# Four edits in a fused four-layer convolution kernel: where a mean is taken off, a fused weighting and sum, the engine that writes zeroes, and the order of small matmuls

## The chip, the cores and the metric

The kernel runs on one core of a Trainium2 chip. The core has TensorE (PE in the profile; its weight loads are shown as PEld), VectorE (DVE), ScalarE (ACT), GpSimd (POOL) and SyncE (SP), which here only issues transfers. The metric is the device time of the whole kernel in microseconds (us), lower is better. The kernel before takes 7199.5 us, the median of 3 runs (7186.45 to 7207.52).

## The reference, cut to what matters

The input x has the shape (16, 32, 128, 128), fp32. Four layers follow, each `x = x + layer(groupnorm(x))`, where the group norm takes mean and variance over 2 channels and all of the image:

```python
x = x + _L0_conv_ref(_gn(x), ...)   # a row LSTM over the skewed image
x = x + _L1_conv_ref(_gn(x), ...)   # "adder" convolution: -sum |patch - w|
x = x + _L2_conv_ref(_gn(x), ...)   # Hartley transform, 32 x 32 modes mixed, back
x = x + _L3_conv_ref(_gn(x), ...)   # five edge filters, normed, then a small U-net
```

The change lies in layers 2 and 3. Layer 2 takes a two-dimensional Hartley transform of the normed image along both axes (a product with cos + sin), keeps the lowest 32 x 32 modes, adds a mirrored and signed copy, multiplies over the 32 input channels for each mode (the mixing), and transforms back:

```python
xm = dht2d(x)[:, :, :m1, :m2]
z = einsum('bixy,ioxy->boxy', xm, yeven) + einsum('bixy,ioxy->boxy', flip(xm), yodd)
out = dht2d(zero_padded(z)) / (h * w)
```

The constant mode of a transform is the plain sum; all its other modes do not see a constant that is added to the image.

Layer 3 starts with five edge filters, each normed by its own mean and standard deviation over the whole image (`b_k = (c_k - mean) / std`). The first convolution works on the five together. The kernel never forms the five filtered images: it takes products of the image's rows with its rows (a Gram matrix), and the variance of each filter is a weighted sum over that matrix. The normed filters are then folded into the weights of the first convolution.

## The kernel before, in words

**Stages.** `stage0` is the LSTM (to about 870 us). `Differences.run` is layer 1: for 16 images, two halves each, 72 differences of 128 x 8192 or 128 x 8320 fp16 elements per half are made, each by DVE (L708) or by ACT (L705), and summed by PE (L595). Layers 2 and 3 (`After`) run for four groups of four images each. The first three groups are woven into layer 1 as background work, the fourth (and what is left of the third) follows when layer 1 has ended, in `drain`. So there are a stage before, a combined stage and a tail.

**What sets the order.** In the combined stage a planner writes the order by hand. It keeps a model of the time of DVE, ACT and PE (`weave.dve`, `weave.act`, `weave.pe`). For each difference it estimates when DVE (2.36 us each) and ACT (7.15 us each) would be done and gives it to one of them. In between it advances `After.work`, a Python generator: what it yields is the time of a PE step (positive), a wait (negative) or a wait for sums, and its steps are emitted when the model says that PE has room. Every background operation adds its cost to the model by hand (`weave.dve += 2.2`). `keep_order` then fixes that order on each engine, so a changed cost moves later work. Where differences have no sum ready, `keep_busy` fills PE with products of zeroes (L625). In the tail `drain` runs the two generators (third and fourth group) side by side by the same model; each engine keeps its own order of instructions.

**Layer 2, `forward(g)`.** `xs` (128 x 4096 fp32) is the right side of the mixing: its two off-diagonal blocks must be zero, and POOL zeroes them (L988, L989). Eight tiles xh of 16 channels are loaded (L997). The group norm's statistics are computed on DVE and PE, spread to all partitions by a product (L1013) and copied to `mr` (L1015: mr[:, 0] the means, mr[:, 1] the inverse deviations). For each tile n: `centred` subtracts the mean from the 128 x 2048 tile in place on DVE (L1019); `first` transforms along the rows on PE (L1066), the result is copied to `ta` (L1070); `turned` transposes it on PE (L1081); `scaled` multiplies by the inverse deviation out of PSUM into t1, 16 channels by 32 modes (L1025); `second` transforms along the other axis (L1036). The modes are copied (L1040), stored to memory (L1046) and read back in another layout into xs and xw (L1119); an addition on DVE makes the mirrored part (L1126, L1133).

**Mixing.** For each of 32 ky, 16 products with 128 x 32 weights and 8 columns (L1154). The product k writes to the 32 partitions of column group j = k // 4 of the result, so four products in a row use the same column group of PE. Each fp32 product shows as two matmuls in the trace. The weights come in 8 tiles of four ky each (L1141). The result is copied (L1171) and stored (L1178).

**Layer 3, `statistics`.** Gram products on PE (L1354) into four PSUM banks, 420 columns each. For each of five filters and four banks the bank is multiplied by a table `gm` (L1414) and the product is summed over its columns (L1415) into `red`. Sums over partitions (L1424), mean, variance and inverse root follow on DVE; then `wf`, the folded weights (L1480, L1482), from tables v that POOL loads (L1467). `conv1` begins with L1627 and L1643, which need wf, and its main work is L1671. ACT normalises the frames that statistics and conv1 read (L1313 with copies at L1317 to L1320); small copies of their sides go to DVE (L1384).

## Time and profile before

The profiled execution has a span of 7206.6 us from its first to its last instruction; that is within the spread of the three runs and 7.1 us above their median.

| what | us |
|---|---|
| median of 3 runs | 7199.5 |
| lowest and highest run | 7186.45, 7207.52 |
| span of the profiled execution | 7206.6 |
| PE busy, in the whole span | 5631.0 |
| DVE busy | 5845.3 |
| ACT busy | 5498.0 |
| POOL busy | 111.8 |
| POOL's zeroing of xs (L988 and L989, eight operations) | 14.6 + 11.3 |

How to read it: busy time is a sum over the whole span and hides that the stages have different limits. In the stretch in which an engine is busy nearly all the time, work taken from it shortens the stretch; in a stretch in which it waits, it does not. So each part of the change has to be placed in its stretch first, and the waits there tell what it frees. The profile is one execution, so its durations are set against its own span.

### The profile page before, as it was taken

How to read it: one execution, taken by the hardware profiler on the slowest of the kernel's cores; microseconds unless marked ns; L12 is line 12 of the kernel's file. 1: busy time of each engine (PE TensorE's matmuls, PEld its weight loads, DVE VectorE, ACT ScalarE, POOL GpSimd, SP SyncE). 2: the span in 40 equal slices, each digit the busy share in tenths (PEclk: the TensorE clock that was granted, in tenths of full speed). 3: DMA queues.
4: the chain of work that ended last, by engine and by line, in shares of the span. 5: the costliest groups of instructions: out<-in, count | busy, mean ns of one | idle time of the engine just before them, and what ended most of it. 6: DMA issues, size and time to landing. Idle time of an engine off the chain costs nothing. (4 is left out here: it accounts for less than half of the span.)

```text
span 7206.6 us, 271424 instructions
## 1 busy us (share of the span) xinstructions
PE 5631.0 (78%) x127740; PEld 3001.3 (42%) x127740; DVE 5845.3 (81%) x7099; ACT 5498.0 (76%) x3100; POOL 111.8 (2%) x91
## 2 busy tenths in 40 slices
PE   4778567777877777998777787999776784797896
PEld 3665333333334343333334343333333443554564
DVE  7787689999998989999998999999998994134224
ACT  2555489999998989999999999999998991131222
POOL 0000000000000000000000001000000000000000
PEclk9899789999988898999888998999888986798997
DMA  8664211111133432221343343221252245252324
GB/s 310 230 205 144 83 63 57 55 58 47 47 101 93 141 98 81 63 69 47 78 126 98 115 118 104 65 65 46 57 134 92 64 136 150 89 170 74 86 51 98
DMA packets 372719, 722.57 MB, mean 100 GB/s; under 512 B 50896, under 2 KB 217296, under 8 KB 360720
## 3 DMA queue, kind: packets, MB, share of 16 engines
q1 hardware_dynamic: 364128, 670.79, 30.6%
q0 software_dynamic: 7040, 33.80, 1.4%
q8 instruction: 999, 16.37, 1.0%
q14 instruction: 120, 0.98, 0.0%
q10 hardware_dynamic: 432, 0.64, 0.0%
HBM read 507.28 MB, written 164.32 MB: 93 GB/s over the span
## 5 line engine op out<-in xcount | busy, mean ns | idle before, releaser
L705 ACT ACTIVATE d_act<-q,neg 128x8192 f16<-128x8192 f16 (+1 forms) x631 | 4462.6, 7143 | 184.4 <-PE acc L595 135.0
L708 DVE TENSOR_SCALAR d_dve<-q,qw 128x8192 f16<-128x8192 f16 (+1 forms) x1673 | 3859.4, 2362 | 200.8 <-PE acc L595 158.0
L595 PE MATMUL acc<-d_dve,sel 128*32 128x512 f16 x26768 | 1869.8, 402 | 504.0 <-DVE d_dve L708 454.0
L595 PEld LDWEIGHTS <-sel 128*32 128x32 f16 x36864 | 1026.9, 100 | 2164.4 <-issue 1507.8
L1671 PE MATMUL acc<-xp,wf 32*32 32x512 f32 x25600 | 1043.7, 618 | 37.6 <-issue 32.8
L595 PE MATMUL acc<-d_act,sel 128*32 128x512 f16 x10096 | 724.4, 408 | 356.2 <-ACT d_act L705 343.6
L1671 PEld LDWEIGHTS acc<-xp,wf 32*32 32x32 f32 x25600 | 431.9, 104 | 416.5 <-issue 329.6
L625 PE MATMUL acc<-q,zero 128*32 128x512 f16 x7248 | 522.9, 401 | 0.0
L1609 ACT ACTIVATE y<-pooled,b 32x128 f32<-32x128 f32 x488 | 195.0, 400 | 414.4 <-DVE pooled L1595 407.8
L207 PE MATMUL pg<-h,wb 64*64 64x20 f32 (+15 forms) x4096 | 395.7, 320 | 106.1 <-DVE h L256 64.8
L852 PE MATMUL acc<-y,u_conv 32*32 32x256 f32 (+1 forms) x9728 | 359.8, 459 | 76.0 <-issue 46.6
L244 ACT ACTIVATE gt<-pg,bias 128x20 f32<-128x20 f32 (+15 forms) x1024 | 315.8, 374 | 80.2 <-PE pg L207 73.1
L1313 ACT ACTIVATE xp<-xp,shift,stats 128x1280 f32<-128x1280 f32 (+1 forms) x128 | 182.6, 1434 | 240.5 <-DMA xp<-x_d 210.1
L207 PE MATMUL pg<-e,wb 64*64 64x20 f32 (+15 forms) x4096 | 353.1, 315 | 16.4 <-DVE e L260 5.4
L207 PEld LDWEIGHTS pg<-h,wb 64*64 64x64 f32 x4096 | 248.3, 154 | 140.7 <-DVE h L256 90.4
L625 PEld LDWEIGHTS <-zero 128*32 128x32 f16 x7248 | 218.6, 102 | 203.0 <-issue 46.1
L207 PE MATMUL pg<-xn,wb 64*64 64x28 f32 (+61 forms) x4096 | 284.5, 302 | 11.3 <-ACT gt L244 3.8
L207 PEld LDWEIGHTS pg<-e,wb 64*64 64x64 f32 x4096 | 251.5, 156 | 92.1 <-DVE e L260 62.9
L1354 PE MATMUL acc<-xp 32*64 32x204 f32 (+3 forms) x8576 | 238.5, 344 | 37.8 <-ACT xp L1319 28.8
L1800 DVE TENSOR_SCALAR s<-acc,l_ms,l_one 128x512 f32<-128x512 f32 x128 | 102.3, 824 | 199.0 <-PE acc L852 199.0
L255 ACT ACTIVATE th<-c 128x20 f32<-128x20 f32 (+15 forms) x256 | 81.3, 320 | 235.5 <-DVE c L253 234.1
L852 PEld LDWEIGHTS acc<-y,u_conv 32*32 32x32 f32 x9728 | 171.4, 110 | 196.6 <-issue 130.4
(215 smaller groups left out, 4303.1 us busy)
## 6 DMA issues: line engine op xcount, KB each, us to landing
xr<-x_d SPq DMA_DIRECT2D x192, 512.0 KB
xp<-x_d SPq DMA_DIRECT2D x112, 640.0 KB
q<-q_d SPq DMA_DIRECT2D x32, 2145.0 KB
x_d<-xr SPq DMA_DIRECT2D x128, 512.0 KB
x_in<-in_x_dram SPq DMA_DIRECT2D x16, 2048.0 KB
res<-in_x_dram SPq DMA_DIRECT2D x64, 512.0 KB
xn<-in_xs_dram SPq DMA_DIRECT2D x64, 512.0 KB
xn<-xn SPq DMA_DIRECT2D x128, 256.0 KB
```

Source lines behind the costliest of these rows:

```text
L207: nc.tensor.matmul(bank[c][q][64 * pair : 64 * pair + 64, :, :width], wb[half, 4 * kind + KIND[q]].rearrange("p b o -> p (b o)"), v[half], ...
L244: nc.scalar.activation(gt[:, q, :, :n], bank[c][q][:, :, :n], AF.Tanh if q == G else AF.Sigmoid, bias=bias[:, KIND[q] : KIND[q] + 1],)
L595: self.nc.tensor.matmul(acc[k][32 * j : 32 * j + 32, :], self.sel16[:, i // 9, :], d[:, row : row + 4, c : c + W], start=first, stop=last,)
L625: self.nc.tensor.matmul(acc[k][32 * j : 32 * j + 32, :], self.zero, q[:, :4, :W], start=False, stop=False)
L705: nc.scalar.activation(dst, src, AF.Relu, bias=self.neg[:, i : i + 1])
L708: nc.vector.tensor_scalar(dst, src, self.qw[:, i : i + 1], 0.0, ALU.subtract, ALU.max)
L852: nc.tensor.matmul(acc[blk][32 * j : 32 * j + 32, o : o + rows * n], t[part, 4 * par + tap, :], src[part, top : top + rows, left : left + ...
L1313: nc.scalar.activation(v, v, AF.Identity, bias=self.shift3, scale=self.stats3[:, 1])
L1354: nc.tensor.matmul(gram[blk][j : j + width, at : at + n], xp[part, l, 2 + j : 2 + j + width], xp[part, rows, j : j + width + 4], start=sta ...
L1609: nc.scalar.activation(d, s, AF.Identity, bias=bj)
L1671: nc.tensor.matmul(acc[blk][32 * j : 32 * j + 32, :], tap_of("all", tap)[rows], xp[rows, 4 * j + kh : 4 * j + kh + 4, kw : kw + W], start= ...
L1800: nc.vector.tensor_scalar(s.rearrange("p r w b -> p b r w"), acc[blk].rearrange("p (b r w) -> p b r w", b=2, w=64), istd[:, blk : blk + 1] ...
```

## The change

- `forward`, zeroes: two ACT activations per group replace the two POOL memsets; each reads one element of a constant over and over (step 0), multiplies it by 0.0 and writes 64 x 2048 elements. The model is charged 4.2 us on ACT.
- `forward`, mean: `centred` is gone. The first transform now sees the raw image. One operation makes mr[:, 0] = mean x 128 x inverse deviation, and after `scaled` a second small operation takes that off column 0 of each channel of t1, the constant mode of the first transform (16 elements on each partition).
- `statistics`: the multiplication and the reduction become one fused operation with an accumulator output; the compiled program has two instructions for it, the operation and a read of the accumulator. The model is charged 0.7 us instead of 1.2.
- `mixing`: the 16 products of one ky are issued in the order 0, 4, 8, 12, 1, 5, ..., so that the column group changes with each product.

```diff
@@ forward @@
-            nc.gpsimd.memset(xs[:64, 4:], 0.0)
-            nc.gpsimd.memset(xs[64:, :4], 0.0)
+            for part, off in ((slice(0, 64), xs[:64, 4:]), (slice(64, 128), xs[64:, :4])):
+                one = cst["ones"][part, 0:1]
+                flat = bass.AP(one.tensor, one.offset, [list(one.ap[0]), [0, 2048]])
+                nc.scalar.activation(off.rearrange("p b k y -> p (b k y)"), flat, AF.Identity, scale=0.0)
+            self.weave.act += 4.2
...
-                def centred(n):
-                    x, cs = xh[n], slice(16 * (n % 2), 16 * (n % 2) + 16)
-                    nc.vector.tensor_tensor(x, x, bcast(mr[:, 0, n // 2, cs], 2, W), ALU.subtract)
-                    weave.dve += 2.2
+
+                nc.vector.scalar_tensor_tensor(mr[:, 0], mr[:, 0], float(H), mr[:, 1], ALU.mult, ALU.mult)
 
                 def scaled(n, p):
                     cs = slice(16 * (n % 2), 16 * (n % 2) + 16)
@@ scaled @@
                         t1, p.rearrange("p (c k) -> p c k", k=M1), bcast(mr[:, 1, n // 2, cs], 2, M1), ALU.mult
                     )
-                    weave.dve += 0.7
+                    nc.vector.tensor_sub(t1[:, :, 0], t1[:, :, 0], mr[:, 0, n // 2, cs])
+                    weave.dve += 0.9
                     t1s[n] = t1
...
                 yield -4.0
-                centred(0)
-                yield -2.5
                 t1s, ta, ready = {}, {}, {}
...
                 for n in range(10):
-                    if n < 7:
-                        centred(n + 1)
                     if n < 8:
                         yield first(n)
@@ mixing @@
-            for k in range(16):
+            for k in [4 * j + i for i in range(4) for j in range(4)]:
                 j = k // 4
                 nc.tensor.matmul(
@@ statistics @@
                 w = pool.tile([128, GRAM], F32, name="es_w", bufs=1)
-                nc.vector.tensor_tensor(w, gram[blk][:, :GRAM], gm[k], ALU.mult)
-                nc.vector.tensor_reduce(red[:, blk, k : k + 1], w, AX.X, ALU.add)
-                weave.dve += 1.2
+                nc.vector.tensor_tensor_reduce(
+                    w, gram[blk][:, :GRAM], gm[k], 1.0, 0.0, ALU.mult, ALU.add, accum_out=red[:, blk, k : k + 1]
+                )
+                weave.dve += 0.7
                 if blk % 2:
                     yield -1.0
```

## The prediction

> **What bounds the kernel now.** I read the page first: its span, the busy shares and the 40 slices.

> ```profile
> span 7206.6 us, 271424 instructions
> ...
> PE 5631.0 (78%) x127740; PEld 3001.3 (42%) x127740; DVE 5845.3 (81%) x7099; ACT 5498.0 (76%) x3100; POOL 111.8 (2%) x91
> ...
> DVE  7787689999998989999998999999998994134224
> ACT  2555489999998989999999999999998991131222
> PEclk9899789999988898999888998999888986798997
> ```

> A slice is 180 us. DVE and ACT stand at 8 to 9 tenths from slice 5 to slice 33 and nearly empty afterwards: two stages with different limits. The start times of L708 and L207 give the borders (last LSTM product near 870 us, last difference near 5943), and the table of stretches gives their sums. Its columns are the stretch, its length, busy time and count of each engine, granted clock, DMA share, GB/s.

> ```profile
> 870.00:5943.40 5073.40, 4056.81 (x85506) 1904.30 (x85510) 4742.43 (x3860) 4801.01 (x1234) 91.48 (x51) 0.92 0.28 83
> 5943.40:7206.60 1263.20, 963.45 (x29938) 622.44 (x29930) 431.75 (x1033) 265.56 (x514) 17.85 (x33) 0.84 0.38 103
> ```

> In the combined stage (5073 us) DVE is busy 93.5% and ACT 94.6%: they share the same differences, so it ends when their joint work ends. In the tail (1263 us) PE works 963 us; it is limited by PE and, where PE is idle, by chains through DVE and DMA. The groups by shape give the prices (us busy, mean ns of one):

> ```profile
> L705 ACT ACTIVATE d_act<-q,neg 128x8192 f16<-128x8192 f16 x451 | 3186.8, 7112 | 155.0 <-PE acc L595 105.7 <-DMA q<-q_d 46.7 <-issue 1.8
> L708 DVE TENSOR_SCALAR d_dve<-q,qw 128x8192 f16<-128x8192 f16 x1085 | 2522.7, 2351 | 162.9 <-PE acc L595 120.9 <-DMA q<-q_d 40.1
> L1154 PE MATMUL acc<-xs,mix 128*32 128x8 f32 x4096 | 103.4, 186 | 46.3 <-DMA mix<-in_mix_dram 15.7 <-DMA q_d<-qt 13.4 <-DVE is_t L759 11.5
> L1019 DVE TENSOR_TENSOR xh<-xh,mr 128x2048 f32<-128x2048 f32 x32 | 72.5, 2285 | 4.2 <-DMA xh<-x_d 4.2
> L1414 DVE TENSOR_TENSOR es_w<-acc,gm 128x420 f32<-128x420 f32 x80 | 47.5, 594 | 12.5 <-PE acc L1354 9.4 <-DVE es_red L1415 0.5
> L1415 DVE TENSOR_REDUCE es_red<-es_w 128x1 f32<-128x420 f32 x80 | 47.2, 590 | 2.5
> ```

> Last the timeline of the tail, where the removed work meets PE's idle time (start, length, engine, instruction, in brackets idle before and what ended it):

> ```profile
> 6011.49 11.10 DVE L1019 TENSOR_TENSOR xh<-xh,mr 128x2048 f32<-128x2048 f32 x5
> 6022.66 6.69 DVE L1019 TENSOR_TENSOR xh<-xh,mr 128x2048 f32<-128x2048 f32 x3
> 6022.82 1.25 ACT L1313 ACTIVATE xp<-xp,shift,stats 128x1024 f32<-128x1024 f32 x1 [4.01 <-DVE sides L1384]
> 6029.42 1.28 DVE L1070 COPY ta<-acc 128x512 f32<-128x512 f32 x2
> 6030.16 1.12 PE L1081 MATMUL acc<-cw,ta 128*128 128x128 f32 x4 [11.76 <-DVE ta L1070]
> ...
> 6118.92 0.61 PE L1424 MATMUL acc<-es_red,cw 128*128 128x20 f32 x2 [26.85 <-DVE es_red L1415]
> 6131.47 11.85 PE L1154 MATMUL acc<-xs,mix 128*32 128x8 f32 x387 [11.53 <-DVE is_t L759]
> 6179.95 0.29 PE L1627 MATMUL acc<-cw,wf 128*32 128x4 f32 x8 [12.74 <-DVE wf L1482]
> 6204.80 10.76 PE L1671 MATMUL acc<-xp,wf 32*32 32x512 f32 x273
> ```

> PE stands behind the mean subtraction, then the Gram sums, then the mixing, then wf; only at 6204.8 does the long run of conv1 begin.

> [...] the trace's L1313 (1024: 1246 ns, 1280: 1461) [...] gives 2.1. [...] L1627 agrees: its eight, over four column groups, take 0.29 us in all.

> **The combined stage.** Counted in the built programs up to the last difference, three groups' transforms and two groups' Gram sums lie here.
> - DVE loses 24 subtractions x 2.285 = 54.8 us and 40 Gram pairs x (0.594 + 0.590) = 47.4, together 102.2.
> - DVE gains 40 fused operations. Nothing in the trace shows one. Lower bound 0.60 (the multiply alone, read hidden), upper 1.2 (half rate over its two streams, 0.594 + 0.44, plus a read of 0.17 like the smallest DVE operations, e.g. L739). I take 0.70, since it reads the same two streams as L1414: 28.0. Further 24 subtractions of 16 columns x 0.17 = 4.1, and three scalings of 128 columns x 0.28 (as L1040) = 0.8.
> - The planner hands 9 differences from ACT to DVE (L708 1682 for 1673, L705 622 for 631): +9 x 2.36 = 21.2 on DVE, -9 x 7.14 = -64.3 on ACT.
> - ACT gains six zeroings x 2.1 = 12.6 and one normalisation with its copies (1.9) that was in the tail.
> - Sum: DVE -102.2 + 54.1 = -48.1; ACT -64.3 + 14.5 = -49.8. Two engines that must end together agree. The fused operations now wait for one another on DVE, so I take **-46**. The idle rest (331 us of DVE) I leave unscaled: most waits are for sums at the borders of units. Bounds: -25 (fused at 1.2) to -58.

> Costed at nothing: the mixing here, because PE is not the limit (its 7248 filler products L625 become 7088); POOL's zeroing, 26 us busy on an idle engine. The zeroes on ACT have no wait of their own here; the differences queued behind them are delayed by what is already summed. If that cover fails (memory not free yet), ACT stalls with all differences behind it.

> **The tail**, by the changed kernel's order of instructions:
> 1. First transform. L1066 no longer needs the mean, and the ta copies come behind only the sides copies. The last of these needs L1313, which waited 4.01 us behind the subtractions; it could start at 6018.8 and be copied at 6021. So ta at about 6021 for 6029.4: **-8.5**. From there xm goes through SP to memory and returns as xs and xw; those DMA times stay, so mixing starts at 6123, not 6131.5.
> 2. Gram: 33 us (6085.3 to 6118.3) become 20 x 0.75 + 5 of other copies = 20, from 6077 to 6097. In the new order the last two mode additions follow the first pieces of wf, no longer inside the Gram block; wf is ready at about 6131.
> 3. Mixing: PE does 392 of 512 products before L1627, in 784 instructions. Before, 1024 took 35.5 us at half clock (30 ns each in the runs). L1627's eight start within 0.11 us, 14 ns each: 784 x 0.014 = 11 us. Bounds: 6 ns (the step between its neighbours) to 30. So L1627 at 6134 for 6180: **-46**. The mix weights of the last eight columns may hold it a little (before, the pair issued at 6135.66 filled the DMA until 6147).
> 4. The other 120 products come between conv1's (+3.5), and z then returns about 17 us after its copy, near 6202, when PE is there: +2.
> 5. Zeroes: ACT writes them near 5968, in a 25 us wait for a frame load; the loads into xs start near 6047. Nothing; with the cover gone, 4.2 us on the frames behind. POOL loses a wait of 61 us, but its next transfers (gm, v) wait for DVE anyway. SP keeps its order but for one frame load.
> 6. Last group's Gram (6579 to 6612) is 9 us shorter, and wf is waited for again (25.6 us in two times, 12.7 shown above); PE has conv2 beside it: -2.

> Sum -46 + 3.5 + 2 - 2, about **-42**. What is late next is PE itself: 201 of 210 us busy from 6240 to 6450. Bounds: -8.5 (only step 1) to -55.

> Together -88. The span, 7206.6, lies 7.1 above the median of the runs and inside their spread; I subtract from the median: 7199.5 - 88 = **7112**.

> **Rivals.**
> - Only the combined stage pays: the tail's DMA round trips decide, as the DVE waits for xw (40 us in 7) suggest; against it, wf and not xw holds L1627. 7199.5 - 46 - 8.5 = 7145.
> - The fused operation costs as much as the pair: 40 x 0.48 = 19 back in the combined stage, 10 in the tail: 7141.
> - Slower: the fused operation is far slower on DVE. The planner charges it 0.7 and would not rebalance, so each excess x over the pair's 1.18 counts 40 times there and 40 in the tail's two chains, against 59 us of other gains. At +22 us, 80x = 81: x = 1.0, or 2.2 us each, decides; at 3.0 the time would be 7199.5 - 59 + 146 = 7286. For it: nothing measured. Against: two ordinary streams.
> - The new order of differences and background work wastes what was saved, in waits for loads: 7180 to 7205.

> **How the numbers follow.** Forecast 0.60 (own range 7085 to 7138), tail without gain 0.20, fused as dear as the pair 0.10, slow fused 0.06, wasted order 0.04. 7075 to 7165 takes in the first three but their ends. Faster by over 0.3% (22 us, about what a measurement here can tell from none): 0.89; within: 0.05; slower: 0.06.

> **What would show it.** L708 at 1682 and the last difference near 5897; the fused group's mean below 0.75 us; no idle PE of 12 us before L1081; L1154's successor at under 15 ns per instruction; conv1 starting about 215 us after the last difference instead of 261. The forecast is wrong if the last difference stays within 15 us of 5943, or if conv1's start moves and the end does not.

## The result, and the profile after

The changed kernel takes 7136.57 us, the median of four runs (7128.47 to 7141.35); the kernel before took 7202.3 us beside it (four runs, 7186.45 to 7207.52). The ratio is 0.9912, with a 95% interval of 0.9898 to 0.9927: faster by about 64 us. The forecast was 7112 with a range of 7075 to 7165, so the side and the range were right and the gain was put 24 us too high. The experiments show that one stage of the forecast was right in size for less good reason than it seemed.

The profiled execution has a span of 7139.6 us, 67.0 less than that of before. The last difference ends at 5900.1 us (before: 5941.5). First the page of after, then the table of stretches with that border (columns as in the prediction):

```profile
span 7139.6 us, 271100 instructions
...
PE 5578.2 (78%) x127580; PEld 2940.1 (41%) x127580; DVE 5753.4 (81%) x7112; ACT 5452.3 (76%) x3099; POOL 81.9 (1%) x83
```

```profile
870.00:5900.10 5030.10, 4016.54 (x85362) 1866.67 (x85366) 4689.13 (x3870) 4752.46 (x1231) 65.18 (x45) 0.92 0.28 84
5900.10:7139.60 1239.50, 947.85 (x29926) 599.86 (x29918) 393.40 (x1038) 269.61 (x516) 14.26 (x31) 0.84 0.39 105
```

Against before, with the same border (5071.5 and 1265.1 us), the combined stage lost 41.4 us and the tail 25.6; the forecast had 46 and 42. In the combined stage DVE's busy time fell from 4742.2 to 4689.1 and ACT's from 4801.0 to 4752.5, while the idle rest (length less busy time) went from 329 to 341 on DVE and from 271 to 278 on ACT.

The groups of after answer to those of before (L705 and L708 here with both widths, 8192 and 8320, in one line):

```profile
L705 ACT ACTIVATE d_act<-q,neg 128x8192 f16<-128x8192 f16 (+1 forms) x622 | 4402.5, 7149 | 182.1 <-PE acc L595 133.3 <-DMA q<-q_d 44.7 <-issue 3.3
L708 DVE TENSOR_SCALAR d_dve<-q,qw 128x8192 f16<-128x8192 f16 (+1 forms) x1682 | 3877.5, 2361 | 168.0 <-PE acc L595 125.5 <-DMA q<-q_d 38.1
L1152 PE MATMUL acc<-xs,mix 128*32 128x8 f32 x4096 | 52.1, 188 | 73.3 <-DVE xs L1131 38.4 <-DMA mix<-in_mix_dram 18.9 <-issue 15.8
L1412 DVE CUSTOM_DVE_ANT_0 es_w<-acc,gm 128x420 f32<-128x420 f32 x80 | 47.5, 593 | 20.2 <-PE acc L1352 9.8 <-DMA gm<-in_gram_dram 7.2 <-DVE es_red L1412 0.5
L991 ACT ACTIVATE xs<-cw 64x2048 f32<-64x2048 f32 x8 | 15.2, 1904 | 11.7 <-DMA x_d<-xr 11.7
L1412 DVE DVE_READ_ACCUMULATOR2_ANT es_red<- 128x1 f32 x80 | 6.6, 82 | 0.0
```

The fused operation takes 593 + 82 ns = 0.675 us (forecast 0.70), a zeroing 1.90 us (forecast 2.1, the line through L1313's two lengths taken to 2048 elements), 1682 differences went to DVE as counted, and the mixing's busy time is half of the 103.4 us of before. Every price was right to within a tenth or so. The fused operation takes as long as the multiplication did (594 ns), so the half rate of the forecast's upper bound did not show; the 0.44 us there is an estimate from the groups of before, 2285 ns for 2048 elements and 594 for 420, so 1.04 ns per element. What was missed is in the tail's mixing. PE there, in order of time:

```profile
6085.79 2.21 PE L1152 MATMUL acc<-xs,mix 128*32 128x8 f32 x148 [38.41 <-DVE xs L1131]
6089.21 1.90 PE L1152 MATMUL acc<-xs,mix 128*32 128x8 f32 x128 [1.22 <-issue]
6095.70 1.90 PE L1152 MATMUL acc<-xs,mix 128*32 128x8 f32 x128 [4.59 <-issue]
6100.27 1.90 PE L1152 MATMUL acc<-xs,mix 128*32 128x8 f32 x128 [2.67 <-issue]
6104.01 1.90 PE L1152 MATMUL acc<-xs,mix 128*32 128x8 f32 x128 [1.85 <-issue]
6107.48 1.83 PE L1152 MATMUL acc<-xs,mix 128*32 128x8 f32 x123 [1.57 <-issue]
6109.11 0.20 PE L1626 MATMUL acc<-cw,wf 128*32 128x4 f32 x2
```

Within a burst a matmul takes 1.90 / 128 = 14.8 ns, as forecast (14). But a full burst is 128 matmuls long and is followed by idle time that no semaphore explains ("issue"). The trace also records transfers of kind "instruction"; in this stretch the view of transfers shows

```profile
q8 instruction: 6, 0.10, 1.6%
```

six packets of 16384 bytes. Those after the first begin at 6093.51, 6097.95, 6101.33, 6105.13 and 6108.61 us, and the bursts from 6095.70 on begin 2.2 to 2.7 us after one of them. In the whole execution the trace has 998 such packets, and PE executed 2 x 127580 = 255160 matmuls and weight loads: 255.7 to a packet, as many as a burst's 128 matmuls with their 128 weight loads. So, by these counts and times, PE takes one packet's worth in 1.9 us and then waits for the next, which comes every 3.5 us at best and after 6.5 us while mix weights load: 784 matmuls took 23.3 us, not 11.

L1626 also needs wf, but wf was not what held it. Its last two pieces are ready at 6104.65 us, 4.5 us before L1626 starts, and they stood in DVE's order behind a copy that itself waited for the mixing's first half:

```profile
6101.97 1.02 DVE L1169 COPY zs<-acc 128x256 f32<-128x256 f32 x2 [8.18 <-PE acc L1152]
6102.84 1.81 DVE L1481 SCALAR_TENSOR_TENSOR wf<-v,ops,wf 128x1152 f32<-128x1152 f32 x2
```

### The profile page after: what moved, and what is told of

Same layout as the page of the kernel before. It is cut to its first block, busy times and chain, and to the rows that moved or that the text cites. A ratio compares the mean times of both kernels' runs of the same rounds, so it can differ in the third digit from the quotient of the medians.

```text
span 7139.6 us, 271100 instructions
## 1 busy us (share of the span) xinstructions
PE 5578.2 (78%) x127580; PEld 2940.1 (41%) x127580; DVE 5753.4 (81%) x7112; ACT 5452.3 (76%) x3099; POOL 81.9 (1%) x83
## 5 line engine op out<-in xcount | busy, mean ns | idle before, releaser
L705 ACT ACTIVATE d_act<-q,neg 128x8192 f16<-128x8192 f16 (+1 forms) x622 | 4402.5, 7149 | 182.1 <-PE acc L595 133.3
L708 DVE TENSOR_SCALAR d_dve<-q,qw 128x8192 f16<-128x8192 f16 (+1 forms) x1682 | 3877.5, 2361 | 168.0 <-PE acc L595 125.5
L595 PE MATMUL acc<-d_dve,sel 128*32 128x512 f16 x26912 | 1877.6, 403 | 507.3 <-DVE d_dve L708 441.5
L595 PEld LDWEIGHTS <-sel 128*32 128x32 f16 x36864 | 1022.7, 100 | 2203.4 <-issue 1547.7
L595 PE MATMUL acc<-d_act,sel 128*32 128x512 f16 x9952 | 720.5, 411 | 376.1 <-ACT d_act L705 368.0
L625 PE MATMUL acc<-q,zero 128*32 128x512 f16 x7088 | 510.1, 399 | 0.0
L207 PE MATMUL pg<-h,wb 64*64 64x20 f32 (+15 forms) x4096 | 397.6, 320 | 102.0 <-DVE h L256 60.7
L207 PE MATMUL pg<-e,wb 64*64 64x20 f32 (+15 forms) x4096 | 353.1, 315 | 18.2 <-DVE e L260 6.3
L207 PEld LDWEIGHTS pg<-h,wb 64*64 64x64 f32 x4096 | 246.0, 153 | 137.5 <-DVE h L256 86.9
L625 PEld LDWEIGHTS <-zero 128*32 128x32 f16 x7088 | 215.0, 102 | 198.4 <-issue 44.7
L207 PE MATMUL pg<-xn,wb 64*64 64x28 f32 (+61 forms) x4096 | 283.6, 302 | 10.9 <-ACT gt L244 3.2
L207 PEld LDWEIGHTS pg<-e,wb 64*64 64x64 f32 x4096 | 250.1, 155 | 96.8 <-DVE e L260 67.6
```

The source lines that it names most:

```text
L207: nc.tensor.matmul(bank[c][q][64 * pair : 64 * pair + 64, :, :width], wb[half, 4 * kind + KIND[q]].rearrange("p b o -> p (b o)"), v[half], ...
L595: self.nc.tensor.matmul(acc[k][32 * j : 32 * j + 32, :], self.sel16[:, i // 9, :], d[:, row : row + 4, c : c + W], start=first, stop=last,)
L625: self.nc.tensor.matmul(acc[k][32 * j : 32 * j + 32, :], self.zero, q[:, :4, :W], start=False, stop=False)
L705: nc.scalar.activation(dst, src, AF.Relu, bias=self.neg[:, i : i + 1])
L708: nc.vector.tensor_scalar(dst, src, self.qw[:, i : i + 1], 0.0, ALU.subtract, ALU.max)
```

## The experiments

Times below are ratios to the kernel before, measured beside it. The microseconds that stand with them come from four sessions, in which before itself took 7198.5 to 7223.4 us, so kernels are compared by their ratios. E is the end of the last difference, read from each kernel's one profiled execution.

### The parts one by one

**e1_old_order**: after without the new order of the mixing.

```diff
-            for k in [4 * j + i for i in range(4) for j in range(4)]:
+            for k in range(16):
```

> The changed kernel with the mixing's products in their old order (sixteen columns of one column group after another). Everything else stays, and 390 products still stand ahead of L1626. Delivery theory (in the tail the mixing waits for its instructions, which arrive as pieces of 16 KB, 128 product instructions each, every 3.5 us or later): the runs of products get twice as long (128 in 3.9 us for 1.9), but the time from the first product to L1626 grows only from 23.3 us to 27-29, conv1 starts 4-6 us later, and the whole kernel takes 7140-7144 us. Rival, the prediction's: products run at their own pace, 784 at 30 ns for 14, so +12.5 us from the first product to L1626 and 7149 or more. Both: the last difference within 3 us of 5898, since PE does not bound the combined stage.

Measured: 0.9921 (0.9908 to 0.9934), 7148.37 us; the interval overlaps that of after. PE in its tail:

```profile
6090.62 8.51 PE L1152 MATMUL acc<-xs,mix 128*32 128x8 f32 x276 [38.86 <-DVE xs L1131]
6100.88 4.00 PE L1152 MATMUL acc<-xs,mix 128*32 128x8 f32 x128 [1.74 <-issue]
6107.09 11.38 PE L1152 MATMUL acc<-xs,mix 128*32 128x8 f32 x374 [2.22 <-issue]
```

128 matmuls take 4.00 us for 1.90, yet the stretch from the first one to L1626 is 27.7 us for 23.3. A factor of two in the pace of PE buys 4.4 us there, and nothing behind it: conv1 starts 230.7 us after E for 231.2, and the tail is 1239.2 us long for 1239.5. The delivery theory holds for the mixing (27 to 29 us expected), the forecast's 12.5 us fall. Its other numbers were missed: conv1 should have started 4 to 6 us later, and the last difference ended at 5907.4 us, 7.3 later than in after (by e5_pool_charged, below, E moves by 13 us with the order unchanged). What stands is this: cycling the column groups moved the limit of the mixing from PE to the delivery of its instructions.

**e2_pair**: after with the Gram's two operations back.

```diff
-                nc.vector.tensor_tensor_reduce(
-                    w, gram[blk][:, :GRAM], gm[k], 1.0, 0.0, ALU.mult, ALU.add, accum_out=red[:, blk, k : k + 1]
-                )
-                weave.dve += 0.7
+                nc.vector.tensor_tensor(w, gram[blk][:, :GRAM], gm[k], ALU.mult)
+                nc.vector.tensor_reduce(red[:, blk, k : k + 1], w, AX.X, ALU.add)
+                weave.dve += 1.2
```

> The changed kernel with the Gram's two operations (multiply, then reduce) in place of the fused one, charged 1.2 as before. Balance theory: each of the 40 in the combined stage is 0.61 us dearer on VectorE, 24.6 us, of which the planner hands two or three differences back to ScalarE, so both engines and the last difference go up by about 17-19 us (5915-5917, L708 at about 1679). In the tail: twice 12 us of VectorE; group 3's chain to conv1 is bound by it (+10), group 2's hardly (+2 to +8), because its wf is done before the mixing is. Sum +29 to +37: 7166-7174 us. Rival (the tail's Gram sums are hidden behind transfers and products in both groups): +18, 7155.

Measured: 0.9964 (0.9952 to 0.9976), 7184.23 us; E at 5918.4, with 1680 differences on DVE. That is 0.0052, or 37 us, more than after; 18 us of it before E, as the balance says: DVE's idle rest is 341 us, that of after. The rest is in the tail, whose order also differs from after's (all 512 products stand ahead of L1626 here), so it can't be put down to the Gram alone.

**e3_mean_only** is the kernel before with the mean's part of the change and nothing else; **e4_pool_zero** is after with one part undone:

```diff
-            for part, off in ((slice(0, 64), xs[:64, 4:]), (slice(64, 128), xs[64:, :4])):
...
-                nc.scalar.activation(off.rearrange("p b k y -> p (b k y)"), flat, AF.Identity, scale=0.0)
-            self.weave.act += 4.2
+            nc.gpsimd.memset(xs[:64, 4:], 0.0)
+            nc.gpsimd.memset(xs[64:, :4], 0.0)
```

> The kernel before with the mean moved to the constant mode, and nothing else: pair, zeroing on GpSimd and old order of the mixing stay. Balance theory: 24 subtractions of 2.285 us less, 5 us of small ones more, some five differences handed over, so the last difference 36-39 us earlier than before's 5941.5 (5903-5906). Tail: the eight subtractions leave the path to the first ta (-8 to -13); conv1 after the last difference at about 252 for 263. Sum -45 to -50: 7152-7157 us. Rival (the tail gains nothing, because the Gram pair keeps VectorE until the same time): -37, 7165.

> The changed kernel with the zeroes written by GpSimd again and ScalarE's 4.2 us charge gone. Balance theory: six zeroings of 1.9 us leave ScalarE, 11.4 us, about one difference moves back to it, both engines and the last difference 2-3 us earlier (about 5895); the tail unchanged within 3 us. 7131-7136 us: the move to ScalarE cost a little. Rival (GpSimd's zeroing holds its later transfers of gm and v, which the tail needs): the tail 4 us or more longer, 7140 or above.

Measured: e3_mean_only 0.9999 (0.9990 to 1.0008), 7207.74 us; e4_pool_zero 0.9996 (0.9987 to 1.0005), 7210.42 us. Both miss by some 50 to 75 us: neither gains anything. And yet the work went away as counted:

| combined stage, from 870 us to E | length | DVE busy, idle | ACT busy, idle |
|---|---|---|---|
| before | 5071.5 | 4742.2, 329 | 4801.0, 271 |
| after | 5030.1 | 4689.1, 341 | 4752.5, 278 |
| e3_mean_only | 5085.3 | 4703.1, 382 | 4766.4, 319 |
| e4_pool_zero | 5092.9 | 4689.2, 404 | 4748.3, 345 |
| e5_pool_charged | 5043.5 | 4693.8, 350 | 4743.2, 300 |
| e6_act_uncharged | 5085.8 | 4686.1, 400 | 4760.3, 326 |
| e7_charge_3p8 | 5057.4 | 4683.6, 374 | 4769.6, 288 |

e3_mean_only has 39 us less work on DVE than before (24 subtractions, less the small operations and five differences handed over, come to 38), but 53 us more idle time. e4_pool_zero has exactly the work of after on DVE and 63 us more idle time. So the balance says how much work there is, and something else how much of the stage stands idle. My theory that balance alone decides had fallen.

### The engine that zeroes, or the order?

The planner writes a new order whenever a charge changes. So e4_pool_zero did two things: it moved the zeroes to GpSimd and, by taking out 4.2 us of charge, it gave every engine another order. Two more kernels take these apart. **e5_pool_charged** is e4_pool_zero with the line `self.weave.act += 4.2` kept; **e6_act_uncharged** is after with that line removed. In the built programs the first has after's order on PE, DVE and SP to the instruction, the second that of e4_pool_zero. **e7_charge_3p8** alters the charge alone, by 0.4 us:

```diff
-            self.weave.act += 4.2
+            self.weave.act += 3.8
```

> The changed kernel with the zeroes written by GpSimd, but with the planner's charge of 4.2 us to ScalarE kept, so that the order of every other instruction on TensorE, VectorE, ScalarE and SyncE is that of the changed kernel. Order theory (what cost 70 us in e4_pool_zero was not GpSimd's writing but the new order that the missing charge brought, which put the stores of xm behind a 2 MB load of q and the mixing ahead of its data): back at the changed kernel's time less what ScalarE saves, 7125-7140 us, last difference 5890-5900. Rival (GpSimd's writing itself disturbs: its queue, or its accesses to memory beside VectorE's): 7180-7210, last difference 5950 or later.

> The counterpart: zeroes by ScalarE as in the changed kernel, but without the charge, so that the order of everything else is that of e4_pool_zero. Order theory: as slow as e4_pool_zero, 7195-7220 us, last difference at about 5960-5970 (ScalarE's 11 us more), with the wait of some 35 us for a store of xm in group 2. Rival (GpSimd's writing disturbs): 7135-7150.

> The changed kernel with the zeroing charged at 3.8 us, which is what the trace shows for two of them, for 4.2. No instruction is added or removed; the planner only puts some of them elsewhere. Order theory: the engines' work stays within 3 us (VectorE about 4690 us busy, ScalarE about 4752 from the first to the last difference), but the idle time lies anywhere between that of the changed kernel (341) and that of e4_pool_zero (404): 7130-7210 us, and a change of over 10 us either way would show that so small a shift decides. Rival (the order matters only where a charge is wrong by several us): within 8 us of the changed kernel, 7130-7145.

Measured:

| | order of after (charge 4.2) | order without the charge |
|---|---|---|
| zeroes by ACT | 0.9912 (0.9898 to 0.9927) | e6_act_uncharged 0.9988 (0.9982 to 0.9995) |
| zeroes by GpSimd | e5_pool_charged 0.9909 (0.9894 to 0.9924) | e4_pool_zero 0.9996 (0.9987 to 1.0005) |

Who writes the zeroes makes no difference that can be told; the order makes 0.0076 to 0.0087, 55 to 63 us. e7_charge_3p8 comes to 0.9982 (0.9974 to 0.9991), 7188.48 us: a charge nearer to the measured 2 x 1.904 us costs 50 us. Of that kernel's longer span 27.3 us lie before E and 18.6 after. Its work did not stay within 3 us as expected: the planner gave three differences more to ACT, which is 17 us busier (DVE 6 us less), and here ACT ends last. In the tail all 1024 matmuls of the mixing stand ahead of L1626, which comes 15.8 us later after E.

Some of the idle time can be read in e6_act_uncharged, at two long waits of its combined stage that after does not have. First SP, which issues the transfers:

```profile
5459.02 1.70 SPq L562 DMA_DIRECT2D q<-q_d  x1
5460.81 6.46 SPq L1047 DMA_DIRECT2D xm_d<-xm  x2
5501.65 0.52 SPq L1116 DMA_DIRECT2D xs<-xm_d  x1
```

DVE meanwhile:

```profile
5465.02 2.35 DVE L708 TENSOR_SCALAR d_dve<-q,qw 128x8192 f16<-128x8192 f16 x1
5501.35 0.29 DVE L1041 COPY xm<-acc 128x128 f32<-128x128 f32 x1 [33.98 <-DMA xm_d<-xm]
```

And later SP again, and then PE:

```profile
5634.88 0.56 SPq L562 DMA_DIRECT2D q<-q_d  x1
5636.33 39.60 SPq L1201 DMA_DIRECT2D zi<-z_d  x4
```

```profile
5646.72 1.05 PE L595 MATMUL acc<-d_dve,sel 128*32 128x512 f16 x16
5676.55 0.48 PE L1215 MATMUL acc<-cw,zi 32*32 32x32 f32 x4 [28.78 <-DMA zi<-z_d]
```

Twice small transfers of the background (stores of 64 KB, loads of 128 KB) were issued right behind a load of q, 2145 KB, in the same queue. The second store landed some 34 us after its issue, and PE had the last of the four loads 40 us after the first was issued. The first time DVE, in its fixed order, waits for the buffer of xm and all its differences with it; the second time PE waits for zi and the sums of the differences behind it wait too. In after's order the same transfers fall into other places: its longest wait for xm's store is 12.4 us, and its list of waits has none for zi. e4_pool_zero, with e6's order, shows both stalls again (35.1 and 29.2 us). In e6 they are 34.0 and 28.8 us, and its DVE idles 59 us more than that of after. That the stalls make up this difference is argued from the sums, not tested, and it goes for this one order: DVE's longest wait for xm's store is 5.7 us in e7_charge_3p8 and 15.0 in e3_mean_only. Why these two idle more stays open.

Why a load of q takes that long: while it flows, the table of stretches (last two columns: share of the 16 DMA engines that is busy, GB/s) shows for e6_act_uncharged (the other columns are the engines' busy time)

```profile
5475.00:5495.00 20.00, 0.00 (x0) 0.00 (x0) 0.00 (x0) 6.04 (x1) 0.00 (x0) 0.50 0.25 73
```

A quarter of 16 engines, as if four were busy. In after, where a load of q flows nearly alone from 5456 to 5470 us (0.25, 107 GB/s), the trace has four of its packets in flight nearly all that time, 17160 bytes and 640 ns (median) each. Why four, no run shows: a load of q cut in another way wasn't tried.

### Two attempts to do better

**e8_mix_later** takes up what holds the start of the mixing: in after, xw of block 2 stands in the queues behind six loads of mix, 1024 KB each.

```diff
+                while weave.draining and len(self.asked) < 4:
+                    yield -2.0
                 wt = [self.weights(wp, i) for i in range(self.buffers["t_w"])]
```

(`asked` is a set to which `modes` adds its block once its loads are issued.)

> The changed kernel with group 3's mixing weights (in the tail alone) asked for after the last block's loads of xs and xw: of the 6 MB that lay ahead of the loads of xs and xw, 2 MB still do. The combined stage keeps its order. Transfer theory (block 2's xw, asked for at E+136 in the changed kernel, E being the end of the last difference, landed only at E+165 because it stood behind 6 MB of mix in the queues, and block 3's store and loads behind it): the mixing starts at E+155 to E+167 for E+186, all 512 products now stand ahead of L1626 and take 30-33 us because of the delivery of instructions, conv1 starts at E+206 to E+220 for E+231 and no products are left inside conv1 (-5): 7105-7120 us. Rival (the round trip through memory takes that long anyway, or the weights, asked for later, are then waited for): 7132-7142.

Measured: 0.9905 (0.9888 to 0.9921), 7130.36 us. The mixing starts at E + 168.8 for E + 185.7, but conv1 at E + 231.7 for E + 231.2:

```profile
6066.84 2.20 PE L1156 MATMUL acc<-xs,mix 128*32 128x8 f32 x149 [22.94 <-DVE xs L1135]
6070.74 1.89 PE L1156 MATMUL acc<-xs,mix 128*32 128x8 f32 x128 [1.70 <-issue]
6076.68 1.90 PE L1156 MATMUL acc<-xs,mix 128*32 128x8 f32 x128 [4.04 <-issue]
6082.89 1.89 PE L1156 MATMUL acc<-xs,mix 128*32 128x8 f32 x127 [4.32 <-issue]
```

This misses the 7105 to 7120 us of the transfer theory. All 1024 matmuls now stand ahead of L1630, after's L1626, and again come 128 at a time (34 us in all; the first four bursts are shown); then wf is waited for (4.4 us), whose last pieces stand in DVE's order behind the copies of the mixing's result. So the slow delivery holds wf as well. conv1's end is at E + 547.8 for E + 569.1; no product is left inside it, but before's conv1 had none either and took 331.6 us, so most of these 21 us has a cause that I haven't followed. At the end of the kernel 9 us are left of it (a tail of 1230.5 for 1239.5). By its interval this version can't be told from after, and no kernel here is surely faster than after.

**e9 to e12** issue the loads of q from ACT's queue, so that nothing small stands behind them in SP's; all else keeps its order.

```diff
-        self.nc.sync.dma_start(q, bass.AP(q_d.tensor, first, ...
+        self.nc.scalar.dma_start(q, bass.AP(q_d.tensor, first, ...
```

> e6_act_uncharged with one thing moved: the 32 loads of q (2145 KB each, L562) are issued by ScalarE, on its own queue, so that SyncE's queue holds no such load ahead of the background's small transfers; all other instructions keep the order of e6_act_uncharged. Queue theory (the two long stalls there, 34 us behind xm's store and 29 us behind the load of zi, came from standing behind a load of q in one queue): both go, and with smaller ones of the kind the time falls by 50-75 us, to 7120-7145. Rival (the 16 DMA engines themselves are full while q is loaded, whichever queue it comes from): stays at 7180-7195.

> The changed kernel with the loads of q on ScalarE's queue, all else in the changed kernel's order. Queue theory: its own waits of this kind are small (12 us for xm's store in group 0, 7 to 8 us several times for xw), so 15-35 us faster: 7100-7122, and within 20 us of e9_q_uncharged, since the place of the background no longer decides. Rival (ScalarE waits at the issue for q's buffer to be free and its differences with it): slower than 7140.

> Both: the loads of q on ScalarE's queue and group 3's mixing weights asked for after the last block's loads. If the two gains are of different stages they add: 6-10 us less than e10_q_after, 7092-7115. Rival: nothing beyond e10_q_after within 3 us.

> The kernel before with the loads of q on ScalarE's queue, all else in its own order. Queue theory: its stalls behind q are few, 10-35 us faster than before, 7165-7190; the difference to e10_q_after is then the change's worth with this source of luck taken out: 50-80 us. Rival (before's order had no such luck, good or bad): as before within 5 us.

Measured: 1.0386 (1.0369 to 1.0403), 1.0385 (1.0366 to 1.0404), 1.0377 (1.0362 to 1.0393) and 1.0459 (1.0436 to 1.0482). All four are some 270 to 330 us slower than the kernel before: a miss for the queue theory's times. Of the rivals' only e10's "slower than 7140" came true, and not for its reason: the semaphore instructions before ACT's loads of q took 38 ns at most. ACT's waits in the combined stage of after and then of e10_q_after (what waits, for what, us in all, times, longest):

```profile
ACT xq L543 <- DMA xq<-x_d: 53.4, 7, 21.4
```

```profile
ACT xq L543 <- DMA xq<-x_d: 315.1, 17, 32.0
```

And ACT at one of them, with the stretch in which both loads flow:

```profile
1519.72 0.53 ACTq L562 DMA_DIRECT2D q<-q_d  x1
1526.65 14.23 ACT L705 ACTIVATE d_act<-q,neg 128x8192 f16<-128x8192 f16 x2
1560.71 1.24 ACT L543 ACTIVATE xq<-xq,shift,r 128x1024 f32<-128x1024 f32 x1 [19.83 <-DMA xq<-x_d]
```

```profile
1527.00:1549.00 22.00, 17.52 (x276) 8.56 (x269) 21.93 (x22) 13.88 (x2) 0.00 (x0) 0.92 0.26 97
```

In after one of the two loads of xq that ACT needs next stood ahead of the load of q, in one queue with it. Now SP issues both from 1517.75 us and ACT the load of q at 1519.72, and with both in flight still only 0.26 of the engines' time is busy, at 97 GB/s. So, by the share, the second queue brought no second path here, and it took away an order that had been right. Nor did the waits that it was to remove go: in e9_q_uncharged DVE still waits up to 21.9 us for xm's store and up to 37.1 for xw. ACT's waits for xq are most of what the stage got longer (262 of 360 us in e10_q_after). It is 5390.5 us long in e10_q_after, 5397.1 in e9_q_uncharged and 5394.8 in e12_q_before, whose DVE has 50 us more work. So the three orders differ by less than 7 us here, but under a new limit. These four therefore say little on the order of the background, and what the change is worth without the luck of an order stays open.

## Why the prediction was right, and where it was wrong

- **Combined stage, prices and balance.** -46 forecast, -41.4 measured. DVE's work fell by 53 us (48 forecast) and ACT's by 48.5 (50). Right.
- **Combined stage, "The idle rest ... I leave unscaled".** It held in this order: 341 us for 329. That it held is the part that was not earned. Less work was worth nothing in e3_mean_only and e4_pool_zero, and 0.4 us of charge cost 50 us in e7_charge_3p8. The rule put before the prediction, that work taken from an engine busy nearly all the time shortens its stretch, failed there, with DVE busy 92% of the stage. The rival "The new order of differences and background work wastes what was saved" had 0.04; three of the five orders without the subtractions that were run (e3_mean_only, that of e4_pool_zero and e6_act_uncharged, and e7_charge_3p8) went its way wholly or mostly. The change's own order (and e2_pair's) did not; nothing that I read beforehand told them apart. That the order drawn was a good one was luck: the chance of faster, 0.89, was too high for what the profile could tell, although the result was on that side.
- **Zeroes.** In the 25 us wait of the tail ACT's zeroing waited 11.7 us itself, and it cost nothing, as forecast; by e5_pool_charged (0.9909 for 0.9912) it costs nothing anywhere that can be told. The wait of POOL that went was worth nothing either.
- **Tail, step 1.** The first ta at E + 74.4 (E + 87.9 before): -13.5 for -8.5.
- **Tail, step 2.** The Gram's sums end at E + 146.3, earlier than the E + 155.5 forecast. The mixing was put at E + 181.5 and starts at E + 185.7.
- **Tail, step 3, "784 x 0.014 = 11 us": the term that failed.** It measured 23.3 us, because PE's pace is that of its instructions' delivery; the kernels whose tail has the same order agree (23.4 us in e5_pool_charged, 22.2 in e6_act_uncharged). With the later start that is 12.3 + 4.2 = 16.5 us; L1626 is at E + 209.0 for the forecast's E + 192.5. The tail's whole shortfall, 42 - 25.6 = 16.4 us, comes out the same in part by chance, since the misses of the next steps nearly cancel. The bounds (6 to 30 ns) held the value, but as a pace of PE; the trace of before had shown the pauses, after 128 and 256 matmuls, and I had read past them.
- **Tail, steps 4 and 6.** conv1, which now has the other products inside it, takes 337.9 us for 331.6, 6.3 more (3.5 + 2 forecast). The last group's chain to conv1 gained a further 10 us where 2 were forecast, and that group's conv1 (340.3 us for 336.0) and what follows it (199.0 for 193.1), which the change does not touch, gave them back.
- **The split is rougher than it looks.** e5_pool_charged, with the order of after, has E at 5913.5 and a tail of 1221.3, 13 later and 18 shorter than after. Read from that kernel the combined stage lost 28.0 us and the tail 43.9: it is then the first that falls short and the second that meets its forecast. The whole is firm, the border between its parts to some 15 us only; the 12 us of step 3 stand in both kernels.

## What to carry to other kernels

Where a planner or a hand-written order ties several engines together, removed work is not yet a gain, since the idle time can take all of it (39 us in e3_mean_only): before crediting an edit, run its charge or its order a little off, and see how much of the time is alignment. A matmul can get faster than the delivery of its own instructions (here 128 matmuls with their weight loads per 16 KB packet, 3.5 us at best): a doubled pace gained 4.4 of 27.7 us here, so count instructions as well as columns. And look for the one long transfer in a queue that carries short ones: here 2145 KB, at a quarter of the DMA engines' time, held up 64 KB for 34 us, and moving it to another queue only moved the collision (ACT's waits for xq in e10_q_after: 315.1 us for 53.4).
